# Gated layer: first projection as a Strassen block product, the second projection one token pair behind

## The chip, the cores and the metric

The kernel runs on one core of one Trainium2 chip. The time is device microseconds of one execution; lower is better. TensorE is called PE here, VectorE DVE, ScalarE ACT, GpSimd POOL, and SyncE, which issues most transfers, SP.

## The reference

One transformer block in float32, for 2 sequences of 1024 tokens and 256 features, with 154 condition tokens a sequence: self-attention, cross-attention, and a gated layer, each behind a layer norm and with a residual. The gated layer, cut to what matters:

```python
h = _layernorm(x, ln3_g, ln3_b)                 # 2 x 1024 x 256
p = h @ ff_w1 + ff_b1                           # 256 -> 2 x 1024
a, gate = (p[..., :D_FF], p[..., D_FF:])        # D_FF = 1024
h = a * jax.nn.gelu(gate, approximate=False) @ ff_w2 + ff_b2
x = h + x                                       # 1024 -> 256
```

## The kernel before

All three layers are written out in one program, and the order of the instructions on each engine is the order of the source. Every engine takes its own instructions strictly in that order. The outer loops run over p (self-attention steps), then c (48 cross-attention steps, three to a head pair), then k (64 slots of the gated layer). Short queues of closures spread the side work over the steps: `side` (the next layer norm, one step at a time), `outs` (pieces of an output projection, name py), `later` (loads and bias adds, L315), `adds`, `stores` and `lates` (what DVE, ACT or POOL do to a result one step later). The last cross-attention work reaches into the gated layer: the final softmax scaling (L824, POOL), transposes (L840, DVE), value products (poc, L876, PE) and their copies (L889, DVE), eight output pieces (L462, PE) with their residual adds (L469, DVE), and the third layer norm of the second sequence: statistics (L235, L236, DVE), deviation (L241, L245, POOL), the offset (L251, DVE), normalizing (L262, POOL), four PE transposes to a pair of token tiles (ph_ln, L275), and two ACT copies with gain and shift (L290).

The gated layer works on transposed activations hT (256 features as two chunks of 128 partitions, tokens along the free axis). A block is 256 tokens of one sequence; there are 8 blocks of 8 slots. `gate_slot(k)` makes one block of 128 features: four PE products of 128x128 weights and 256 tokens, two that sum up the gate half and two the linear half, in two halves of one PSUM tile pa from the pool ps_s (tiles of two banks of 512 float32, two of them). ACT applies Gelu with bias to the gate half (L964), then DVE adds the bias to the linear half and multiplies (L967) into u. `sum_slot()` comes at most some slots later: it multiplies that feature block with the second weights, one product for each of the two token tiles of the block, into two running sums (pf, pool ps_o, two banks). After the eighth feature block DVE adds each sum to the residual x (L993), and the result is stored. A float32 product is two weight loads and two matmul instructions on PE.

PSUM has two more banks in the pool ps_m (`mm_tile`). Before the change the gated layer's products don't use it; the output pieces, the value products and the norm's transposes do. SBUF tiles with the tag P (pool pp_) have six buffers.

The weights are laid out once, w1 as 2 chunks x 2048 columns, w2 as 8 blocks x 256, in one SBUF tile wf that is loaded in the cross-attention.

Of the kernel before, what the change touches and what calls it, by code (L numbers as in the profile page):

```python
# [8 lines left out]
F32 = mybir.dt.float32  # L9
AF = mybir.ActivationFunctionType  # L10
# [3 lines left out]
P = 128  # L14
# [4 lines left out]
def tile_transformer_block(ctx: ExitStack, tc: tile.TileContext, a: dict, out: bass.AP):  # L19
# [13 lines left out]
    GT = 4  # L33
# [884 lines left out]
            flush(stores)  # L918


    NBL = NT // TF
    FF = B * NBL * NF
    gated, sums = [], {}

    def hold_gated():

        wf = pt_.tile([P, 2 * NK, QH // 2], F32, tag="pT", name="wf").rearrange("p a b -> p (a b)")
        n1, n2 = NC * 2 * DF, NF * D
        w1 = wf[:, :n1].rearrange("p (c f) -> p c f", c=NC)
        w2 = wf[:, n1:n1 + n2].rearrange("p (f d) -> p f d", f=NF)  # L930
        pTc["pairs"] = wf[:, n1 + n2:n1 + n2 + 2 * NM * 2 * NT * KB].rearrange(
            "p (a m j q) -> p a m j q", a=2, m=NM, j=2)

        def part1(c, f):
            nc.sync.dma_start(out=w1[:, c, f:f + HB], in_=w["ff_w1"][c * P:(c + 1) * P, f:f + HB])

        def part2(f):
            nc.sync.dma_start(
                out=w2[:, f:f + 2, :],
                in_=w["ff_w2"][f * P:(f + 2) * P, :].rearrange("(f p) d -> p f d", p=P),  # L940
            )

        parts = [lambda c=c, f=f: part1(c, f) for c in range(NC) for f in range(0, 2 * DF, HB)]
        parts.extend(lambda f=f: part2(f) for f in range(0, NF, 2))
        return w1, w2, parts

    def gate_slot(k):

        blk, f = divmod(k, NF)
        b, t0 = divmod(blk * TF, NT)  # L950
        b1 = row_of["ff_b1"]
        h = hT["ff", b]
        if f == 0:
            sums[blk, "u"] = pt_.tile([P, NF, TF * P], F32, tag="V", name=f"u{blk}")
        pa = ps_s.tile([P, 2, HB], F32, tag="s", name=f"pa{k}")
        for half in (1, 0):
            for c in range(NC):
                nc.tensor.matmul(  # L958
                    pa[:, half, :TF * P],
                    lhsT=w1[:, c, half * DF + f * P:half * DF + (f + 1) * P],  # L960
                    rhs=h[:, c, t0 * P:(t0 + TF) * P], start=(c == 0), stop=(c == NC - 1),
                )
        gate = pp_.tile([P, TF * P], F32, tag="P", name=f"gate{k}")
        nc.scalar.activation(  # L964
            gate, pa[:, 1, :TF * P], AF.Gelu, bias=cols[:, b1 + NF + f:b1 + NF + f + 1]
        )
        nc.vector.scalar_tensor_tensor(  # L967
            sums[blk, "u"][:, f, :], pa[:, 0, :TF * P], cols[:, b1 + f:b1 + f + 1], gate,
            op0=ALU.add, op1=ALU.mult,
        )  # L970
        gated.append(k)

    def sum_slot():

        k = gated.pop(0)
        blk, f = divmod(k, NF)
        b, t0 = divmod(blk * TF, NT)
        if f == 0:
            sums[blk] = [sum_tile(f"pf{blk}_{i}") for i in range(TF)]
        for i in range(TF):  # L980
            nc.tensor.matmul(  # L981
                sums[blk][i][:, :D], lhsT=sums[blk, "u"][:, f, i * P:(i + 1) * P], rhs=w2[:, f, :],
                start=(f == 0), stop=(f == NF - 1),
            )
        if f < NF - 1:
            return None

        def store():
            n = TF if blk < B * NBL - 1 else 1
            for i in range(0, TF, n):  # L990
                for t in range(t0 + i, t0 + i + n):
                    xs = xt[b, t // GT][:, t % GT, :]
                    nc.vector.tensor_tensor(xs, sums[blk][t - t0][:, :D], xs, ALU.add)  # L993
                t = t0 + i
                (nc.scalar if i else nc.sync).dma_start(
                    out=out[b, t * P:(t + n) * P, :].rearrange("(t p) d -> p t d", p=P),
                    in_=xt[b, t // GT][:, t % GT:t % GT + n, :],
                )

        return store  # L1000


    with tc.manual_schedule():
# [98 lines left out]
        for c in range(CA):  # L1102
            if c == 0:
                pTc["ring"] = pt_.tile(
                    [P, 2 * NK, QH // 2], F32, tag="pT", name="pT_ca"
                ).rearrange("p a b -> p (a b)")[:, :3 * 2 * NB * NT * KB].rearrange(
                    "p (u n j q) -> p u n j q", u=3, n=NB, j=2)
            if c == SH + 1:
                out_pieces("sa", B - 1, NQ - 1, out_order("sa"))
            if c == SH + 1:  # L1110

                w1, w2, parts = hold_gated()
                add_biases("ca", 0)
# [24 lines left out]
            if c == 0:  # L1138
                drain.append(scale_groups(*joins.pop(0)))
            if c == 2:  # L1140
                turn_groups(SA - 1)
            cross_drain(c)
            if c == 1:
                run(lambda: cross_queries(*nxt))
            elif c == 2:
                run(lambda: cross_queries(*units[2], bank=sum_tile))
            elif c == 3:
                run(lambda: self_values(2 * NU - 1, 0))
            elif c == 4:
                run(lambda: self_values(2 * NU - 1, 1))  # L1150
            elif n == 0 and ui:
                if nxt:
                    run(lambda: cross_queries(*nxt))
                else:
                    run_work(2, 0)
                run_work(0, 1)
            elif n == 1:

                spare["turned"] = True
                run_work(0, 1, sum_tile if outs else None)  # L1160
                flush(stores)
                run_work(0, 0, n_sum=1)
                if ui % 2 == 0:
                    run(lambda: context_values(*units[ui]))
                run_work(1, 0)
                flush(adds)
                flush(stores)
                cross_weigh(c)
            elif n == 2:
                run_work(0, 1, sum_tile if ui == HP + 1 else None)  # L1170
                if c == SH + 1:
                    run_work(2, 0)
                elif ui == HP:
                    wo["ca"] = const.tile([P, NPAIR, D], F32, tag="wo", name="ca_wo")
                    later[:0] = [lambda i=i: nc.sync.dma_start(
                        out=wo["ca"][:, i, :], in_=w["ca_wo"][i * P:(i + 1) * P, :])
                        for i in range(NPAIR)]
            cross_regroup(c)
            for _ in range(min(2, len(later))):
                later.pop(0)()  # L1180

        spare["turned"] = False
        for k in range(FF):
            c = CA + k
            flush(adds)
            gate_slot(k)
            flush(stores)
            flush(lates)
            if k == 2 * len(CG) + 1:
# [1 line left out]
            if k == 0:  # L1191
                out_pieces("ca", B - 1, NQ - 2, out_order("ca"))
            cross_drain(c)
            cross_weigh(c)
            cross_regroup(c)
            if k == len(CG) + 2:
                out_pieces("ca", B - 1, NQ - 1, out_order("ca"))
            if k > len(CG) + 1:

                for _ in range(min(2, len(gated) - (1 if k < FF - 2 else 2))):  # L1200
                    run(sum_slot)
                flush(stores)

            run_work(0 if k == 1 else 2, 1)
            if later:
                later.pop(0)()
        while gated:
            run(sum_slot)
            flush(stores)


# [30 lines left out]
```

## Time and profile before

| | us |
|---|---|
| median of 3 runs | 1107.47 |
| lowest, highest | 1107.26, 1108.68 |
| span of the profiled execution, first to last instruction | 1106.7 |
| first product of the gated layer's first projection (L958) in it | starts at 915.1 |
| first product of the second projection (L981) | starts at 939.1 |

The profile is one execution. Its span covers the instructions alone; what lies around it in a timed run is not in the profile, so the median stands 0.8 us above the span. Groups of instructions are named by line, engine, operation and tiles (out<-in); PEld is the weight load of PE. For each group the profile gives busy time, the mean of one in ns, and the idle time of the engine just before it with the instruction that ended it.

### The profile page before, as it was taken

The page shows a single profiled execution, that of the slowest core. Times are in us where ns is not written, and L with a number is a line of the kernel's source. Part 1 is how long each engine was busy: PE and PEld are TensorE (multiplying, and loading weights), DVE is VectorE, ACT ScalarE, POOL GpSimd, SP SyncE. Part 2 cuts the span into 40 slices and gives each one's busy share as a digit, 9 for nine tenths or more (in the row PEclk, how much of TensorE's full clock was granted, in tenths as well). Part 3 has the DMA queues.
Part 4 walks back from the last instruction along what each step waited for, and adds up shares of the span by engine and source line. Part 5 has one row for each costly group of instructions (what it writes and reads, how often), then busy time and mean ns, then how long its engine had stood idle before and what let it go on. Part 6 is the DMA issues. An engine that isn't in the chain of part 4 may idle for free.

```text
span 1106.7 us, 44775 instructions
## 1 busy us (share of the span) xinstructions
PE 1088.1 (98%) x18452; PEld 721.6 (65%) x18452; DVE 854.5 (77%) x1205; ACT 624.6 (56%) x2025; POOL 662.2 (60%) x1456
## 2 busy tenths in 40 slices
PE   8999999999999999999999999999999999999998
PEld 6555656556756556566565565466776778888887
DVE  5899999898988999999999989868777885322222
ACT  4666666766666666667666766655556552121111
POOL 2766777777778777777777767666656653220000
PEclk9999999999999999999999999999999999999999
DMA  2222212121112022011111111136766553000000
GB/s 82 71 58 53 58 29 52 41 53 42 34 42 49 16 47 49 14 42 33 32 42 33 33 33 27 34 88 163 163 157 139 116 113 77 10 11 10 20 10 20
DMA packets 103982, 60.72 MB, mean 55 GB/s; under 512 B 32218, under 2 KB 94562, under 8 KB 103778
## 3 DMA queue, kind: packets, MB, share of 16 engines
q1 hardware_dynamic: 102546, 57.20, 21.8%
q8 instruction: 146, 2.39, 0.9%
q10 hardware_dynamic: 1232, 0.66, 0.2%
q14 instruction: 58, 0.48, 0.1%
HBM read 27.91 MB, written 2.10 MB: 27 GB/s over the span
## 4 chain that ended last, share of the span: by engine, by line
PE 70%; ACT 8%; DMA 7%; DVE 5%; POOL 4%; SPq 3%; issue 3%; DVEq 0%; POOLq 0%; ACTq 0%
PE po L534 13%; PE s L488 12%; PE pa L958 10%; ACT p L499 7%; DMA st<-st 6%; PE pf L981 5%; PE py_ca L462 5%; PE pq_ca L357 4%; PE poc L876 4%; PE py_sa L462 4%; SPq L509 3%; DVE st L649 3%; PE pv_sa L388 3%; PE sc L797 3%; PE pk_sa L357 3%
## 5 line engine op out<-in xcount | busy, mean ns | idle before, releaser
L499 ACT ACTIVATE p<-s,st 128x512 f32<-128x512 f32 x512 | 344.9, 686 | 196.6 <-DVE st L649 192.8
L599 POOL TENSOR_SCALAR p<-p,rd,ee 128x512 f32<-128x512 f32 x512 | 385.7, 768 | 48.3 <-DVE rd L595 47.4
L649 DVE TENSOR_REDUCE st<-s 128x2 f32<-128x1024 f32 x256 | 300.8, 1216 | 24.9 <-PE s L488 12.7
L613 DVE STREAM_TRANSPOSE pT<-p 128x1024 f32<-128x1024 f32 x256 | 302.4, 1219 | 0.2 <-POOL p L599 0.2
L488 PE MATMUL s<-k_sa,q_sa 64*32 64x512 f32 x4096 | 258.7, 592 | 7.2 <-ACT p L499 6.2
L534 PE MATMUL po<-pT,v_sa 64*32 64x256 f32 x8192 | 240.5, 378 | 1.7 <-DVE pT L613 1.4
L534 PEld LDWEIGHTS po<-pT,v_sa 64*32 64x32 f32 x8192 | 172.5, 107 | 78.7 <-issue 23.7
L488 PEld LDWEIGHTS s<-k_sa,q_sa 64*32 64x32 f32 x4096 | 80.6, 106 | 112.2 <-ACT p L499 51.6
L813 ACT ACTIVATE p<-sc,neg 128x154 f32<-128x154 f32 x256 | 96.1, 403 | 85.1 <-DVE rden L821 80.0
L824 POOL TENSOR_SCALAR p<-p,rden 128x154 f32<-128x154 f32 x256 | 96.8, 398 | 73.7 <-DVE rden L821 73.4
L967 DVE SCALAR_TENSOR_TENSOR u<-pa,cols,gate 128x256 f32<-128x256 f32 x64 | 31.0, 484 | 123.1 <-ACT gate L964 123.1
L958 PE MATMUL pa<-hT_ln,wf 128*128 128x256 f32 x512 | 121.1, 380 | 0.0
L964 ACT ACTIVATE gate<-pa,cols 128x256 f32<-128x256 f32 x64 | 30.3, 474 | 147.5 <-PE pa L958 144.2
L958 PEld LDWEIGHTS pa<-hT_ln,wf 128*128 128x128 f32 x512 | 96.7, 190 | 13.8 <-issue 0.9
L499 ACT ACTIVATION_READ_ACCUMULATOR p<-s,st 128x1 f32 x512 | 104.0, 203 | 0.0
L522 POOL TENSOR_TENSOR zz<-ee,st 128x8 f32<-128x8 f32 x128 | 25.9, 202 | 75.4 <-ACT ee L520 75.4
L388 PEld LDWEIGHTS pv_sa<-sa_wv,hT_ln 64*128 64x128 f32 x1024 | 58.8, 188 | 14.3 <-issue 5.0
L981 PE MATMUL pf<-wf,u 128*128 128x256 f32 x256 | 64.7, 379 | 0.0
L388 PE MATMUL pv_sa<-sa_wv,hT_ln 64*128 64x128 f32 x1024 | 62.0, 275 | 0.0
L462 PE MATMUL py_sa<-sa_wo,o_sa 128*128 128x256 f32 x256 | 59.7, 386 | 0.0
L462 PE MATMUL py_ca<-ca_wo,o_ca 128*128 128x256 f32 x256 | 59.7, 381 | 0.0
L462 PEld LDWEIGHTS py_sa<-sa_wo,o_sa 128*128 128x128 f32 x256 | 47.3, 190 | 17.8 <-ACT v_sa L397 5.9
(88 smaller groups left out, 1230.0 us busy)
## 6 DMA issues: line engine op xcount, KB each, us to landing
wf<-pT_ca SPq DMA_DIRECT2D x128, 128.0 KB, 2.4
st<-st SPq DMA_DIRECT2D x512, 1.0 KB, 1.8
v_sa<-v_sa SPq DMA_DIRECT2D x32, 256.0 KB, 3.8
sa_wq<-in_L_xattn_sa_wq_dram SPq DMA_DIRECT2D x32, 128.0 KB, 3.3
sa_wk<-in_L_xattn_sa_wk_dram SPq DMA_DIRECT2D x32, 128.0 KB, 2.7
sa_wv<-in_L_xattn_sa_wv_dram SPq DMA_DIRECT2D x32, 128.0 KB, 3.5
ca_wq<-in_L_xattn_ca_wq_dram SPq DMA_DIRECT2D x32, 128.0 KB, 3.9
wf<-in_L_xattn_ff_w_dram SPq DMA_DIRECT2D x12, 256.0 KB
```

Of the source, the lines that this page charges most:

```text
L388: nc.tensor.matmul(pv[r][:, i * P:(i + 1) * P], lhsT=h[own, c, i * P:(i + 1) * P], rhs=wt[own, c, :], start=(c == 0), stop=(c == NH - 1), ...
L462: nc.tensor.matmul(py[:, e * D:(e + 1) * D], lhsT=o[:, i, (t + e) * P:(t + e + 1) * P], rhs=wo[kind][:, g * HP + i, :], start=(i == 0), st ...
L488: nc.tensor.matmul(sc[a4 * KB:(a4 + 1) * KB, j, :], lhsT=q[r, c:c + KB], rhs=k[r, h * HB:(h + 1) * HB], start=True, stop=True, tile_positi ...
L499: nc.scalar.activation(pr[:, j, :], sc[:, j, :], AF.Exp, bias=st[:, 0, 0, i, j:j + 1], accum_out=st[:, 0, 1, i, j:j + 1],)
L534: nc.tensor.matmul(po[a2][d:d + KB, :QH // 2], lhsT=v[r, t, e, d:d + KB], rhs=pT[r, d // DH * NK + n, :], start=(t == 0 and e == 0), stop= ...
L599: nc.gpsimd.tensor_scalar(pr[:, j, :], pr[:, j, :], rd[:, c:c + 1], ee[:, 0, c:c + 1], op0=ALU.mult, op1=ALU.mult,)
L613: nc.vector.transpose(halves[h][:, :, c:c + KB], groups.pop(0).rearrange("p j (n k) -> p (j n) k", k=KB))
L649: nc.vector.tensor_reduce(st[:, 0, 0, i, :], sc[i], AX.X, ALU.max, negate=True)
L813: nc.scalar.activation(pr_[:, j, i, :T], sc[:, j, i * T:(i + 1) * T], AF.Exp, bias=neg[:, j, i:i + 1], accum_out=den[:, j, i:i + 1],)
L824: nc.gpsimd.tensor_scalar(pr_[:, j, i, :T], pr_[:, j, i, :T], rden[:, j, i:i + 1], 1.0, op0=ALU.mult, op1=ALU.mult,)
L958: nc.tensor.matmul(pa[:, half, :TF * P], lhsT=w1[:, c, half * DF + f * P:half * DF + (f + 1) * P], rhs=h[:, c, t0 * P:(t0 + TF) * P], star ...
L981: nc.tensor.matmul(sums[blk][i][:, :D], lhsT=sums[blk, "u"][:, f, i * P:(i + 1) * P], rhs=w2[:, f, :], start=(f == 0), stop=(f == NF - 1),)
```

## The change

The first projection is computed for 512 tokens of a sequence at a time (a pair of 256-token halves, 4 pairs, 8 feature blocks each: 32 units). For one feature block the gate and linear halves of the weights, the two feature chunks and the two token halves form a 2x2 block product. It is made with seven products (`product`, numbered 1 to 7) where there were eight. To that end:

- POOL makes sums and differences of the weights in the cross-attention's last 16 steps (`weight_sums`, 16 sums of 128x256; one of the three kinds is written back into w1), and for each pair four sums of token blocks are made (`token_sums`): by DVE for the first pair, at the end of the last cross-attention step, by POOL for the others, half a pair ahead.
- The loop has 64 half units. `gate_first(n)` issues product 1 into a bank of ps_m (pa), which ACT copies to SBUF (own 0); then, by `gate_last(n - 1)`, product 4 of the unit before; then 6 and 5 into the two halves of a ps_s tile pb, to each of which DVE adds own 0 (L1018, L1020). `gate_second(n)` accumulates product 2 onto pa (Gelu by ACT, L1032), product 7 onto the first half of pb (DVE adds own 2 and the bias, L1034), product 3 onto the second half (DVE, L1037; Gelu by ACT, L1038); POOL multiplies into u (L1039). Product 4 accumulates onto the first half of pb once more, DVE takes it (L1046), and POOL multiplies (L1048).
- The second projection starts when a pair's eight units are done, and runs through the next pair's units, two products a half unit, one token tile after the other; the last pair's 32 products come after the loop. Each token tile is added and stored by itself (L1071, L1072).
- u is kept for whole pairs, in the buffers of the tags V and oT and, once, over kT.
- `cross_weigh` runs only in the second half of a unit, and the side work's share of ps_m banks alternates between one and two a step.

```diff
+    def product(n, i, into, first):
+        pair, f = divmod(n, NF)
+        own = slice(f * P, (f + 1) * P)
+        lhs = {
+            1: w1[:, 0, 1, own], 2: w1[:, 1, 1, own], 3: wsum[4][:, own], 4: w1[:, 1, 0, own],
+            5: wsum[1][:, own], 6: wsum[2][:, own], 7: w1[:, 0, 0, own],
+        }[i]
+        nc.tensor.matmul(
+            into[:, :BT], lhsT=lhs, rhs=wh[pair][i], start=first, stop=True,
+            skip_group_check=True)
+
+    def gate_first(n):
...
+        own = pp_.tile([P, 4, BT], F32, tag="P", name=f"own{n}")
+        pa, pb = mm_tile(f"pa{n}"), ps_s.tile([P, 2, HB], F32, tag="s", name=f"pb{n}")
+        psum[n] = (pa, pb[:, 0, :], pb[:, 1, :], own)
+        product(n, 1, pa, True)
+        nc.scalar.copy(own[:, 0, :], pa[:, :BT])
+        if n:
+            gate_last(n - 1)
+        product(n, 6, psum[n][1], True)
+        nc.vector.tensor_tensor(own[:, 1, :], psum[n][1][:, :BT], own[:, 0, :], ALU.add)
+        product(n, 5, psum[n][2], True)
+        nc.vector.tensor_tensor(own[:, 2, :], psum[n][2][:, :BT], own[:, 0, :], ALU.add)
+
+    def gate_second(n):
...
+        product(n, 2, pa, False)
+        nc.scalar.activation(own[:, 3, :], pa[:, :BT], AF.Gelu, bias=bg)
+        product(n, 7, pb, False)
+        nc.vector.scalar_tensor_tensor(
+            own[:, 2, :], pb[:, :BT], ba, own[:, 2, :], op0=ALU.add, op1=ALU.add)
+        product(n, 3, pc, False)
+        nc.vector.tensor_tensor(own[:, 1, :], pc[:, :BT], own[:, 1, :], ALU.add)
+        nc.scalar.activation(own[:, 1, :], own[:, 1, :], AF.Gelu, bias=bg)
+        nc.gpsimd.tensor_tensor(ub[pair][1][:, f, :], own[:, 2, :], own[:, 1, :], ALU.mult)
+
+    def gate_last(n):
...
+        product(n, 4, pb, False)
+        nc.vector.scalar_tensor_tensor(
+            own[:, 0, :], pb[:, :BT], biases(n)[0], own[:, 0, :], op0=ALU.add, op1=ALU.add)
+        nc.gpsimd.tensor_tensor(ub[pair][0][:, f, :], own[:, 0, :], own[:, 3, :], ALU.mult)
+        if f == NF - 1:
+            sums.extend((pair, i, e) for i in range(2 * TF) for e in range(NF))
...
-        for k in range(FF):
+        for k in range(2 * FU):
             c = CA + k
             flush(adds)
-            gate_slot(k)
+            (gate_second if k % 2 else gate_first)(k // 2)
...
-            cross_weigh(c)
+            if k % 2:
+                cross_weigh(c - 1 if k == len(CG) + 2 else c)
...
-            if k > len(CG) + 1:
-                for _ in range(min(2, len(gated) - (1 if k < FF - 2 else 2))):
-                    run(sum_slot)
-                flush(stores)
-            run_work(0 if k == 1 else 2, 1)
+            if k % (2 * NF) == NF and k < 2 * FU - 2 * NF:
+                token_sums(k // (2 * NF) + 1, nc.gpsimd)
+            for _ in range(min(2, len(sums))):
+                run(sum_slot)
+            flush(stores)
+            run_work(0 if k == 1 else 1 + k % 2, 1)
             if later:
                 later.pop(0)()
-        while gated:
+        gate_last(FU - 1)
+        while sums:
             run(sum_slot)
             flush(stores)
```

More of the change, by code (lines that the diff above doesn't have):

```diff
@@ L918, in cross_weigh @@
             flush(stores)
-    NBL = NT // TF
-    FF = B * NBL * NF
-    gated, sums = [], {}
+    NPR = B * 2
+    BT = S // 4
+    FU = NPR * NF
+    wsum, wh, ub, psum = {}, {}, {}, {}
     def hold_gated():
@@ L928, in hold_gated @@
         n1, n2 = NC * 2 * DF, NF * D
-        w1 = wf[:, :n1].rearrange("p (c f) -> p c f", c=NC)
+        w1 = wf[:, :n1].rearrange("p (c h f) -> p c h f", c=NC, h=2)
         w2 = wf[:, n1:n1 + n2].rearrange("p (f d) -> p f d", f=NF)
@@ L932, in hold_gated, with part1 @@
             "p (a m j q) -> p a m j q", a=2, m=NM, j=2)
-        def part1(c, f):
-            nc.sync.dma_start(out=w1[:, c, f:f + HB], in_=w["ff_w1"][c * P:(c + 1) * P, f:f + HB])
+        def part1(c, h, f):
+            f0 = h * DF + f
+            nc.sync.dma_start(out=w1[:, c, h, f:f + HB], in_=w["ff_w1"][c * P:(c + 1) * P, f0:f0 + HB])
         def part2(f):
@@ L941, in part2 @@
             )
-        parts = [lambda c=c, f=f: part1(c, f) for c in range(NC) for f in range(0, 2 * DF, HB)]
+        parts = [
+            lambda c=c, h=h, f=f: part1(c, h, f)
+            for c in range(NC) for h in range(2) for f in range(0, DF, HB)
+        ]
         parts.extend(lambda f=f: part2(f) for f in range(0, NF, 2))
         return w1, w2, parts
[L947 to L951, printed above, removed]
-        h = hT["ff", b]
-        if f == 0:
[L954 to L965, printed above, removed]
-        )
[L967 to L984, printed above, removed]
+    def weight_sums(n):
+        if n == 0:
+            for i in (1, 2):
+                wsum[i] = p2.tile([P, DF], F32, tag="KT", name=f"w1s{i}")
+        if n == DF // (2 * P):
+            wsum[4] = p2.tile([P, DF], F32, tag="QT", name="w1s4")
+        f = n * 2 * P % DF
+        own = slice(f, f + 2 * P)
+        (g0, a0), (g1, a1) = ([w1[:, c, h, own] for h in (1, 0)] for c in range(NC))
+        s1, s2 = wsum[1][:, own], wsum[2][:, own]
+        tt = nc.gpsimd.tensor_tensor
+        if n < DF // (2 * P):
+            return [
+                lambda: tt(s1, a0, a1, ALU.add),
+                lambda: tt(s2, s1, g0, ALU.subtract),
+                lambda: tt(a0, g0, a0, ALU.subtract),
+            ]
+        return [lambda: tt(wsum[4][:, own], g1, s2, ALU.subtract)]
@@ new lines, in token_sums @@
+    def token_sums(pair, engine):
+        b, t0 = divmod(pair * 2 * BT, S)
+        h = hT["ff", b]
+        own = [[h[:, c, t0 + j * BT:t0 + (j + 1) * BT] for j in range(2)] for c in range(NC)]
+        t = pp_.tile([P, 3, BT], F32, tag="P", name=f"hs{pair}")
+        engine.tensor_tensor(t[:, 0, :], own[0][1], own[0][0], ALU.subtract)
+        engine.tensor_tensor(t[:, 1, :], own[1][1], t[:, 0, :], ALU.subtract)
+        engine.tensor_tensor(own[0][1], own[1][1], own[0][1], ALU.subtract)
+        engine.tensor_tensor(t[:, 2, :], own[1][0], t[:, 1, :], ALU.subtract)
+        wh[pair] = {
+            1: own[0][0], 2: own[1][0], 3: own[1][1], 4: t[:, 2, :],
+            5: t[:, 0, :], 6: t[:, 1, :], 7: own[0][1],
+        }
@@ new lines, in product @@
+    def product(n, i, into, first):
[9 more added lines that the diff above has]
+    def gate_first(n):
+        pair, f = divmod(n, NF)
+        if f == 0:
+            one_u = pt_.tile([P, NF, BT], F32, tag="oT" if pair % 2 else "V", name=f"u{pair}_0")
+            if pair == 0:
+                other = kT.rearrange("p a b -> p (a b)")[:, :NF * BT].rearrange(
+                    "p (f t) -> p f t", f=NF)
+            else:
+                other = pt_.tile([P, NF, BT], F32, tag="oT" if pair % 2 else "V", name=f"u{pair}_1")
+            ub[pair] = (one_u, other)
+        own = pp_.tile([P, 4, BT], F32, tag="P", name=f"own{n}")
[9 more added lines that the diff above has]
+        nc.vector.tensor_tensor(own[:, 2, :], psum[n][2][:, :BT], own[:, 0, :], ALU.add)
@@ new lines, in biases @@
+    def biases(n):
+        c = row_of["ff_b1"] + n % NF
+        return cols[:, c:c + 1], cols[:, c + NF:c + NF + 1]
+    def gate_second(n):
+        pair, f = divmod(n, NF)
+        pa, pb, pc, own = psum[n]
+        ba, bg = biases(n)
+        product(n, 2, pa, False)
[7 more added lines that the diff above has]
+        nc.gpsimd.tensor_tensor(ub[pair][1][:, f, :], own[:, 2, :], own[:, 1, :], ALU.mult)
@@ new lines, in gate_last, with sum_slot @@
+    def gate_last(n):
+        pair, f = divmod(n, NF)
+        pa, pb, pc, own = psum.pop(n)
+        product(n, 4, pb, False)
[4 more added lines that the diff above has]
+            sums.extend((pair, i, e) for i in range(2 * TF) for e in range(NF))
+    sums, summed = [], {}
+    def sum_slot():
+        pair, i, f = sums.pop(0)
+        if f == 0:
+            summed[pair] = sum_tile(f"pf{pair}_{i}")
+        own = summed[pair]
+        j, e = divmod(i, TF)
+        nc.tensor.matmul(
+            own[:, :D], lhsT=ub[pair][j][:, f, e * P:(e + 1) * P], rhs=w2[:, f, :],
+            start=(f == 0), stop=(f == NF - 1),
+        )
@@ L985, in sum_slot @@
         if f < NF - 1:
             return None
+        b, t = divmod(pair * 2 * TF + i, NT)
         def store():
[L989 to L998, printed above, removed]
+            xs = xt[b, t // GT][:, t % GT, :]
+            nc.vector.tensor_tensor(xs, own[:, :D], xs, ALU.add)
+            (nc.scalar if pair == NPR - 1 and i % 2 else nc.sync).dma_start(
+                out=out[b, t * P:(t + 1) * P, :], in_=xs)
@@ L1180, in tile_transformer_block @@
                 later.pop(0)()
+            if c == CA - 16:
+                weighted = [fn for n in range(4) for fn in weight_sums(n)]
+            if CA - 16 <= c < CA - 4:
+                weighted.pop(0)()
+            elif c >= CA - 3:
+                for n in {CA - 3: (4,), CA - 2: (5, 6), CA - 1: (7,)}[c]:
+                    weight_sums(n)[0]()
+            if c == CA - 1:
+                token_sums(0, nc.vector)
         spare["turned"] = False
-        for k in range(FF):
+        for k in range(2 * FU):
             c = CA + k
             flush(adds)
-            gate_slot(k)
+            (gate_second if k % 2 else gate_first)(k // 2)
             flush(stores)
```

## The prediction

> **What bounds the kernel now.** I read the busy shares first, then the slices, then the costliest groups of the stage that changes, then its timeline.
>
> ```profile
> PE 1088.1 (98%) x18452; PEld 721.6 (65%) x18452; DVE 854.5 (77%) x1205; ACT 624.6 (56%) x2025; POOL 662.2 (60%) x1456
> ...
> PE   8999999999999999999999999999999999999998
> ...
> DVE  5899999898988999999999989868777885322222
> ...
> POOL 2766777777778777777777767666656653220000
> PEclk9999999999999999999999999999999999999999
> ```
>
> PE is busy in every slice. In the last eight slices, the gated layer, DVE and POOL have little to do. There the matrix engine alone sets the time.
>
> ```profile
> L967 DVE SCALAR_TENSOR_TENSOR u<-pa,cols,gate 128x256 f32<-128x256 f32 x64 | 31.0, 484 | 123.1 <-ACT gate L964 123.1
> L958 PE MATMUL pa<-hT_ln,wf 128*128 128x256 f32 x512 | 121.1, 380 | 0.0
> L964 ACT ACTIVATE gate<-pa,cols 128x256 f32<-128x256 f32 x64 | 30.3, 474 | 147.5 <-PE pa L958 144.2
> ```
>
> The first projection is 256 products, each two PE instructions. PE never idles before one of them (0.0). DVE and ACT wait for PE, never PE for them: the pa tile gets its four products before anything reads it.
>
> ```profile
> 1042.88 1.89 PE L958 MATMUL pa<-hT_ln,wf 128*128 128x256 f32 x8
> 1044.60 1.03 PE L981 MATMUL pf<-wf,u 128*128 128x256 f32 x4
> 1045.47 1.89 PE L958 MATMUL pa<-hT_ln,wf 128*128 128x256 f32 x8
> ```
>
> A slot of 12 instructions takes 1045.47 - 1042.88 = 2.59 us. An instruction thus costs 0.216, a product 0.431, and a result lands 0.379 after its start (the row above says 380).
>
> **What is removed.** Seven products for eight over 512 tokens and 128 features: 32 products fewer of 256, 64 instructions x 0.216 = -13.8 us. The second projection keeps its 128 products. At the end one add and one store follow the last product instead of two adds (0.86 in the timeline for the pair): -0.4. Together **-14.2**.
>
> **What is added: waits of PE for DVE inside a unit.** A unit (one feature block of one 512-token pair) runs on PE as products 1, 4 of the unit before, 6, 5, two second-projection products, 2, 7, 3, two more. Product 6 fills one bank of the tile pb (two banks), 5 the other; DVE reads both (L1018, L1020); 7 and 3 accumulate onto them and are read again (L1034, L1037); then 4. In the built order, with its semaphore counts, product 5 waits for L1018, which reads product 6's bank, not its own. Likewise 7 waits for L1020, 3 for L1034, 4 for L1037. The tile is guarded as one, so neighbouring products alternate with DVE instead of streaming.
>
> [...]
>
> Price of one such turn, from PE's last start: 0.379 to the result; 0.05 until DVE starts (a result at 17.18 is taken by DVE at 17.25); 0.418 for an add from PSUM (the x<-pf,x row) or 0.484 for the three-operand form (L967); 0.12 until PE's next weight load (a DVE copy ends at 17.67, PE loads at 17.79); 0.10 until that load lets the product run (a lone group of eight lasts 1.99, a streaming one 1.89). Sum 1.07 or 1.13; streaming would have taken 0.216. So 3 after 7 loses 0.92. 5 after 6 loses 0.85, and as DVE handles product 4's result first, 0.07 more: 0.92. Waits of 7 and 4 come after 0.216 + 0.86 + 0.43 = 1.51 of other PE work where second-projection products stand between, and cost nothing. A unit so takes 22 x 0.216 + 1.84 = 6.6 us against 5.17 for two slots now.
>
> - **Units 8 to 31** (with second projection): 24 x 1.84 = **+44.2**.
> - **Units 4 to 7** have no second projection between, since it starts when the first pair is complete. All four waits bite: 0.92 + 0.42 + 0.92 + 0.42 = 2.68 a unit, 10.7. There the last norms run too. Their transposes use the same PSUM pair as product 1, and ACT empties them only behind the second Gelu. So product 1 of units 6 and 7 waits for add 0.418, Gelu 0.474 and the two copies (1.01 by the hT_ln rows of L290): with result, hand-overs and restart (0.379, 0.14, 0.22) 2.64 from product 3's last start, less 0.22 and 0.44 of PE work, 1.98 each, and spares a 0.42. 10.7 + 3.96 - 0.84 = **+13.8**. POOL too has a chain there: 1.6 until its first input, then four token sums, five products and a bias add at 0.73 (the x<-x,ff_b row), four times 0.90 for the deviations (0.19 + 0.71) and four times 1.10 to normalize: 16.9 us from the start of unit 4 to the last transpose. A streaming PE would be there after 21 products and three transposes, 10.4; the PE slowed as above comes at about 20, so POOL adds nothing.
> - **Units 0 to 3.** Product 6 needs token sums that DVE makes behind the transposes ending at 917.23: two adds at 0.418 (no row has both inputs in SBUF; 0.3 to 0.45 bounds them), to 918.1, plus restart 0.22, where PE would come at 915.6: 2.7. The rest of unit 0: 0.9 (product 5), 0.2, and 1.3 (product 3's reader behind two transposes). After the next weighing product 1 waits for a copy out of its bank: 0.85; the last out pieces now stand right behind their weighing: 0.9. Three units at 1.84: 5.5. Sum **+12.4**.
> - **Weight sums:** 16 POOL sums x 0.73 = 11.7 us in the last 16 cross steps, hidden: POOL waits 53.5 us there for reciprocals. Uncovered, the four in the last three steps would cost up to 3. I take 0. No DMA is added before the end; 16 small stores take the place of 8 with SP's queue empty.
>
> Extra DVE work a unit (five PSUM reads, 2.2 us), ACT (1.3) and POOL (1.5) fit in 6.6 us.
>
> **Sum:** -14.2 + 44.2 + 13.8 + 12.4 = +56.2 on the span of 1106.7: 1162.9. The median of the runs, 1107.47, lies 0.8 above the profiled span: **1163.7 us**, 5% slower.
>
> **Bounds.** No row shows a turn inside an accumulation. If the weight load runs ahead and the restart is nearly free (0.05 for 0.22), a turn loses 0.17 less: 1.5 a unit, and some 70 turns less 12 us: 1152. If DVE's adds run 10% longer beside POOL and the weight sums bite: 2.0 a unit, 5 more, 3 more, and the POOL chain adds 5: 1177. I take the middle, as the restart rows are of this kernel's own PE.
>
> **Would the clock fall?** PE would have a quarter of its time idle in gaps under 1 us.
>
> ```profile
> 32.00:36.00 4.00, 2.41 (x48) 0.75 (x40) 2.55 (x4) 2.38 (x8) 1.69 (x6) 1.00 0.21 59
> ```
>
> The row is a stretch of 4 us near the start (PE, PEld, DVE, ACT, POOL busy, then the granted clock): PE busy 60%, clock 1.00. So I price no loss. [...]
>
> **Rivals.**
> - *PE keeps streaming* (faster): the reads always end before the next product, so only the -14.2 stays: 1093.3. For it: DVE is idle most of the stage. Against it: product 5 starts 0.216 after 6's last instruction, while a read needs 0.85. It decides where a turn loses under 14.2 / 64 = 0.22 us instead of 0.92.
> - *Only true bank conflicts bind* (no change): if the cross-bank waits cost nothing, POOL's chain becomes the limit of units 4 to 7 (16.9 - 10.4 = 6.5, and 1.98 for ACT's copies) and the start stays (2.7 + 0.85 + 0.9): 1107.5 - 14.2 + 8.5 + 4.5 = 1106.3. Against: the waits are in the program.
> - *Turns half hidden*: 1.0 a unit, 1130 to 1150, if weight loads and decode overlap fully and DVE starts at once. The rows at 17.2 to 17.8 speak against.
> - *The clock drops* in the gaps: if a quarter of the stage's 448 + 256 instructions took double, 176 x 0.216 = 38 more, 1202; with less or more of it 1180 to 1230. The 32 to 36 us row speaks against; its stretch is short.
>
> **How the numbers follow.** Main case 0.80, half hidden 0.08, clock 0.07, streaming 0.03, no change 0.02. The range 1150 to 1180 takes the bounds, leaving out 0.20. Slower by over 0.2% (2.2 us, about what a measurement here can tell) is 0.95, within 0.02, faster 0.03.
>
> **What would show it.** In the profile after: the idle of PE or its weight loads before the products' line released by L1018 and L1034, some 28 us each; steps of 6.6 us from one unit to the next in the late stretch; second-projection products still at 0.216; PE busy near three quarters of the last slices; DVE no longer waiting for ACT but PE for DVE. Steps of 4.7 us would prove me wrong on the waits, steps of 5.7 on their price, a granted clock below 0.95 on the clock.

## The result, and the profile after

The changed kernel takes **1168.47 us** (median of four runs, 1164.85 to 1175.66) beside 1108.08 for the kernel before in the same comparison: a ratio of 1.055, interval 1.052 to 1.059, or 60.4 us more. The forecast was 1163.7 with a range of 1150 to 1180, and slower with a chance of 0.95.

The busy shares and slices of the changed kernel's profile (its span of 1173.9 us is that of the slowest of the four runs):

```profile
PE 1110.9 (95%) x18388; PEld 717.6 (61%) x18388; DVE 899.2 (77%) x1305; ACT 638.2 (54%) x2057; POOL 731.7 (62%) x1548
...
PE   8999999999999999999999999999999887888888
...
DVE  4889999898899999999999898787787643333332
...
PEclk9999999999999999999999999999999896999999
```

PE runs 64 instructions less than before, and yet it is no longer busy throughout: from slice 32 on it stands at seven or eight tenths, with no other engine near its limit. Two slices show a granted clock below nine tenths, which the profile of before has nowhere.

Three of PE's groups from unit 8 on (1001 to 1174 us). The last column is PE's idle time just before the group and what ended it:

```profile
L1061 PE MATMUL pf<-wf,u 128*128 128x256 f32 x224 | 55.0, 379 | 0.0
L995 PE MATMUL pb<-hs,w1s 128*128 128x256 f32 x96 | 31.5, 410 | 14.1 <-DVE own L1018 14.1
L995 PE MATMUL pb<-hT_ln,w1s 128*128 128x256 f32 x48 | 16.8, 431 | 13.8 <-DVE own L1034 13.8
```

Before, PE never idled ahead of a product of the first projection. Here all of its idle time ends with two reads by DVE: L1018, which holds up product 5, and L1034, which holds up product 3. These are the two waits that the prediction named. They are 14 us each on PE, and 24.1 and 23.5 on its weight loads, where the prediction looked for some 28 each. The second projection (L1061) still has none. One such turn, from the timeline of all engines:

```profile
1015.32 0.59 PE L995 MATMUL pb<-hs,w1s 128*128 128x256 f32 x2
1015.52 0.48 DVE L1046 SCALAR_TENSOR_TENSOR own<-pb,cols,own 128x256 f32<-128x256 f32 x1 [0.44 <-PE pb L995]
1016.02 0.42 DVE L1018 TENSOR_TENSOR own<-pb,own 128x256 f32<-128x256 f32 x1
...
1016.50 0.30 PEld L995 LDWEIGHTS pb<-hs,w1s 128*128 128x128 f32 x2 [0.99 <-DVE own L1018]
1016.50 0.70 PE L995 MATMUL pb<-hs,w1s 128*128 128x256 f32 x2 [0.59 <-DVE own L1018]
```

Product 6 starts at 1015.32, its second instruction 0.216 later, at 1015.54. DVE first finishes with product 4 (L1046), then reads product 6's bank until 1016.44. Only then does product 5 start, at 1016.50, though it writes the other bank. From the last start to the next are 0.96 us where streaming has 0.216, and a group behind such a restart lasts 0.70 for 0.59. One turn so costs 0.75 + 0.11 = 0.86 us. A unit with its two turns takes 6.45 us (product 5 at 1010.05 and at 1016.50).

Where the clock fell, in windows (start and end, length, PE's busy time and instructions, granted clock, DMA share, GB/s): units 0 to 3, 4 to 7, and 8 to 31.

```profile
918.77:965.53 46.76, 38.36 (x221) 0.89 0.20 42
965.53:1000.22 34.69, 26.25 (x73) 0.65 0.00 0
1000.22:1156.28 156.06, 128.13 (x530) 0.99 0.03 10
```

Units 8 to 31 lost next to nothing to the clock (0.99); units 4 to 7 ran 24 of their 35 us at half clock.

To see where the time went, the gated layer can be cut at the first products of units 4 and 8, as the timelines give them. The first row is worked out: the 191.6 us of before less 64 x 0.2156; of it 24 x 22 x 0.2156 = 113.8 and the 17.6 from the last product 4 to the end for units 8 to 31, and 28 x 0.431 + 4 x 0.44 (a group of four transposes in the profile of before) for units 4 to 7. The second adds the stalls of the prediction. The others are measured, in microseconds.

| | units 0–3 | units 4–7 | unit 8 to the end | sum |
|---|---|---|---|---|
| streaming (worked out) | 32.6 | 13.8 | 131.4 | 177.8 |
| predicted | 45.0 | 27.6 | 175.2 | 247.8 |
| changed kernel, this profile | 46.8 | 34.7 | 173.7 | 255.1 |
| changed kernel, second profile (e7_after) | 45.7 | 28.4 | 172.7 | 246.8 |
| one-bank tiles (e1_single) | 43.1 | 24.3 | 131.5 | 198.9 |
| sums and norm moved (e2_early) | 45.8 | 22.7 | 173.2 | 241.7 |
| both (e3_both) | 42.6 | 14.7 | 132.4 | 189.7 |
| both and the start (e5_start), from the end of the last scores | 33.5 | 14.7 | 132.5 | 180.7 |

The table compares the gated layer alone, because its start moves from profile to profile, in no order that follows the edits: 915.1 us before, 918.8 in the changed kernel, 914.3 in its second profile. The kernel before took 1111.18 us beside e1 to e4, 1109.08 beside e5 to e7 and 1108.76 beside e8. Ratios are therefore given, each to the kernel before beside the same runs.

### The profile page after: what moved, and what is told of

It is laid out like the page before. It is cut to its first block, busy times and chain, and to the rows that moved or that the text cites. A ratio compares the mean times of both kernels' runs of the same rounds, so it can differ in the third digit from the quotient of the medians.

```text
span 1173.9 us, 44881 instructions
## 1 busy us (share of the span) xinstructions
PE 1110.9 (95%) x18388; PEld 717.6 (61%) x18388; DVE 899.2 (77%) x1305; ACT 638.2 (54%) x2057; POOL 731.7 (62%) x1548
## 4 chain that ended last, share of the span: by engine, by line
PE 61%; DVE 10%; ACT 9%; DMA 7%; POOL 6%; SPq 4%; issue 4%; DVEq 0%; POOLq 0%; ACTq 0%
PE s L488 10%; PE po L534 10%; ACT p L499 8%; PE pb L995 7%; DMA st<-st 6%; PE pf L1061 5%; PE py_ca L462 4%; PE pq_ca L357 4%; DVE st L649 4%; PE poc L876 3%; SPq L509 3%; PE py_sa L462 3%; PE pv_sa L388 3%; PE sc L797 3%; PE pa L995 3%
## 5 line engine op out<-in xcount | busy, mean ns | idle before, releaser
L499 ACT ACTIVATE p<-s,st 128x512 f32<-128x512 f32 x512 | 345.4, 687 | 195.7 <-DVE st L649 189.7
L649 DVE TENSOR_REDUCE st<-s 128x2 f32<-128x1024 f32 x256 | 300.9, 1216 | 25.4 <-PE s L488 10.5
L488 PE MATMUL s<-k_sa,q_sa 64*32 64x512 f32 x4096 | 262.3, 594 | 9.0 <-ACT p L499 8.0
L1039 POOL TENSOR_TENSOR u<-own 128x256 f32<-128x256 f32 x24 | 17.5, 728 | 99.6 <-ACT own L1038 99.6
L1032 ACT ACTIVATE own<-pa,cols 128x256 f32<-128x256 f32 x32 | 15.2, 474 | 101.9 <-PE pa L995 101.9
L995 PE MATMUL pb<-hs,w1s 128*128 128x256 f32 x128 | 45.0, 435 | 21.4 <-DVE own L1018 18.9
L357 PE MATMUL pq_sa<-hT_ln,sa_wq 64*32 64x512 f32 (+1 forms) x976 | 59.3, 594 | 0.0
L357 PE MATMUL pq_ca<-hT_ln,ca_wq 64*128 64x512 f32 (+1 forms) x304 | 58.6, 590 | 0.3 <-DVE rden L821 0.3
```

What stands on the lines that cost most here:

```text
L357: nc.tensor.matmul(pq[r][f:f + m, at:at + n], lhsT=wt[own, c, f:f + m], rhs=h[own, c, t0:t0 + n], start=(c == 0), stop=(c == NH - 1), tile ...
L488: nc.tensor.matmul(sc[a4 * KB:(a4 + 1) * KB, j, :], lhsT=q[r, c:c + KB], rhs=k[r, h * HB:(h + 1) * HB], start=True, stop=True, tile_positi ...
L499: nc.scalar.activation(pr[:, j, :], sc[:, j, :], AF.Exp, bias=st[:, 0, 0, i, j:j + 1], accum_out=st[:, 0, 1, i, j:j + 1],)
L649: nc.vector.tensor_reduce(st[:, 0, 0, i, :], sc[i], AX.X, ALU.max, negate=True)
L995: nc.tensor.matmul(into[:, :BT], lhsT=lhs, rhs=wh[pair][i], start=first, stop=True, skip_group_check=True)
```

## The experiments

**e1_single: is it the guard of the two-bank tile?** From unit 2 on the halves of pb are tiles of their own:

```diff
-        pa, pb = mm_tile(f"pa{n}"), ps_s.tile([P, 2, HB], F32, tag="s", name=f"pb{n}")
-        psum[n] = (pa, pb[:, 0, :], pb[:, 1, :], own)
+        pa = mm_tile(f"pa{n}")
+        if n < 2:
+            pb = ps_s.tile([P, 2, HB], F32, tag="s", name=f"pb{n}")
+            psum[n] = (pa, pb[:, 0, :], pb[:, 1, :], own)
+        else:      # the pool ps_s is closed here, ps_g: four tiles of one bank
+            psum[n] = (pa, *(ps_g[0].tile([P, HB], F32, tag="g", name=f"{name}{n}")
+                             for name in ("pb", "pc")), own)
```

> The changed kernel with one edit: from the third unit on, the two halves of pb are two separate one-bank tiles, so that product 5 no longer waits for the read behind product 6, nor 3 for the read behind 7. Theory (the guard of the two-bank tile costs most of the loss): units 8 to 31 lose 24 x 1.7 us of idle and come at about 4.75 us a unit where the changed kernel took 6.45; what is left is the start (some 8 us) and the norm's POOL chain in units 4 to 7 (some 8 us), so 1107.5 - 14.2 + 8 + 8 + 0.9 = about 1110, up to 1120 if the granted clock still falls there. Rival (the stalls come from PE and DVE sharing the two banks of one tile's region or from DVE itself, not from the guard): steps stay near 6.4 us and the time stays at 1160 or more. Rival (half of the gain is lost to new waits on the own bank): steps of 5.5 us, about 1130.

Measured: 1119.29 us, ratio 1.007 (1.005 to 1.009). PE's groups from unit 8 on, the same two products as above:

```profile
L997 PE MATMUL pc<-hT_ln,w1s 128*128 128x256 f32 x50 | 14.9, 379 | 0.0
L997 PE MATMUL pc<-hs,w1s 128*128 128x256 f32 x48 | 14.3, 379 | 0.0
```

The idle time of 28 us is gone to the last tenth, and a unit takes 4.75 us (its first products at 1040.26 and 1045.01). So the waits of these units were the guard's alone: the same instructions in the same order, with PE writing one bank while DVE reads another, take 4.75 us where 22 x 0.2156 = 4.74 is streaming. What is left of the loss stands in units 0 to 7. In units 4 to 7, two rows of PE's timeline show it:

```profile
968.25 0.33 PE L277 MATMUL ph_ln<-ident,xn_ln 128*128 128x128 f32 x1 [3.88 <-POOL xn_ln L264]
...
974.08 0.70 PE L997 MATMUL pa<-hT_ln,wf 128*128 128x256 f32 x2 [1.33 <-ACT hT_ln L292]
```

The turns between PE and DVE had hidden POOL's chain of sums and norm steps. Without them PE reaches the transposes 3.9 us early, and the copies of ACT hold up product 1 of the next unit.

**e2_early: the other costs alone.** pb stays one tile. The moves:

```diff
-            if c == CA - 1:
+            if c == CA - 2:
                 token_sums(0, nc.vector)
...
-            if k % (2 * NF) == NF and k < 2 * FU - 2 * NF:
+            if k in (3, 24, 40):
...
-            run_work(0 if k == 1 else 1 + k % 2, 1)
+            if k < 8:
+                run_work(0 if k == 1 else 1 + k % 2, 1)
+            else:
+                run_work(1 + k % 2, k % 2, sum_tile if k < 16 else None)
```

> The changed kernel with pb as it is, but the other costs moved: the first pair's token sums one cross-attention step earlier, the second pair's sums in slot 3 in place of 8, the last norm one step every second slot from slot 8, with its transposes in the second projection's idle banks up to slot 15. Theory (the guard carries most of the loss, the start and the norm the rest): units 8 to 31 stay at 6.45 us; 1 to 2.5 us go at the start and 5 to 8 in units 4 to 7, and where the long PE idles go, the stretches at half the granted clock go with them (some 8 to 15 us of the changed kernel's runs): 1145 to 1160. Rival (start and norm chain carry most of the loss): below 1130. Rival (the bank waits alone bring the clock down): stretches at half clock remain in units 4 to 7, 1155 to 1165.

Measured: 1161.58 us, ratio 1.045 (1.043 to 1.046), just above the range expected. Units 8 to 31 did not move. Units 4 to 7, in windows:

```profile
963.49:986.22 22.73, 16.66 (x66) 1.00 0.00 0
```

They fell by 12 us against the first profile of the changed kernel and by 5.7 against the second, and the clock stays full there though all four bank waits remain. So here the bank waits alone did not bring the clock down (1.00), and the norm and its sums cost nothing behind unit 7. Units 0 to 3 gained 1 us against the first profile and nothing against the second, where 1 to 2.5 were expected, and the half clock at the start stayed, for two windows. Product 5 of unit 0 waits 3.55 us there, for the reason that the next run shows.

**e3_both.** The two edits together.

> Both edits together: one-bank tiles from the third unit, and token sums and norm steps moved. Theory: only the removed products and the rest of the start stay, 1107.5 - 14.2 + 5 + 1 + 0.9 = about 1100, between 1096 and 1106, faster than before the change; units at 4.75 us throughout. Rival (another engine or own-bank waits become the bound): units above 5.2 us and 1107 or more.

Measured: 1111.25 us, ratio 1.000 (0.998 to 1.001), a miss: units 4 to 31 run as expected, but the start did not mend. The timeline of the start, some rows:

```profile
918.99 0.83 DVE L981 TENSOR_TENSOR hs<-hT_ln,hs 128x256 f32<-128x256 f32 x1
...
920.42 0.79 DVE L804 TENSOR_REDUCE neg<-sc 128x4 f32<-128x616 f32 x1
...
921.30 0.39 ACT L815 ACTIVATE p<-sc,neg 128x154 f32<-128x154 f32 x1 [3.40 <-DVE rden L823]
...
922.77 0.38 ACT L1021 COPY own<-pa 128x256 f32<-128x256 f32 x1
...
923.19 0.42 DVE L1025 TENSOR_TENSOR own<-pb,own 128x256 f32<-128x256 f32 x1 [0.77 <-ACT own L1021]
...
923.67 1.22 PE L997 MATMUL pb<-hs,w1s 128*128 128x256 f32 x2 [3.03 <-DVE own L1025]
```

The sums, one step earlier, now stand in front of DVE's maximum of the last scores (L804, L802 before), which begins at 920.42; in the changed kernel it began 0.12 us after the start of unit 0's first product, here 1.86. The last exponentials come later by that, the copy of product 1 (L1021) stands behind them on ACT, and product 5 behind the read that needs the copy. The wait of 2.5 us for the sums became one of 0.7, but product 5's wait grew from 0.6 to 3.0: the step had been moved to a worse place in DVE's queue.

**e4_wsums: are the weight sums free?** The kernel before, with the 16 POOL sums added at their places:

```diff
+            if c == CA - 16:
+                weighted = [fn for n in range(4) for fn in weight_sums(n)]
+            if CA - 16 <= c < CA - 4:
+                weighted.pop(0)()
+            elif c >= CA - 3:
+                for n in {CA - 3: (4,), CA - 2: (5, 6), CA - 1: (7,)}[c]:
+                    weight_sums(n)[0]()
```

> The kernel before with the 16 sums of weights added on POOL at the places where the changed kernel has them, into tiles that nothing reads. Theory (POOL waits there for reciprocals, the sums are hidden): 1107.5, within 0.5. Rival (the sums delay the scaling of the last softmax steps): 1109 to 1111, with PE waiting for transposes that wait for POOL in the last three cross-attention steps.

Measured: 1111.68 us beside 1111.18, ratio 1.0005 (0.9992 to 1.0018). The gated layer starts at 918.5 there and takes 191.7 us, as before. A cost of more than 2 us is excluded, one of 0.5 is not.

**e5_start: the two edits and a start put in order.** The first pair's sums are made behind the fourth cross-attention step from the end, unit 0 has its two sums in two tiles of ps_s, and ps_g opens with unit 1. Further:

```diff
+            if k == 0:
+                out_pieces("ca", B - 1, NQ - 2, out_order("ca"))
+                run_work(1, 1, sum_tile)
...
-            if k == 0:
-                out_pieces("ca", B - 1, NQ - 2, out_order("ca"))
             cross_drain(c)
             if k % 2:
                 cross_weigh(c - 1 if k == len(CG) + 2 else c)
+            if k == 1:
+                gate_last(0)
```

> Both edits of the last run, and the start rearranged: the first pair's token sums four cross-attention steps before the end, one output piece and the last transposes ahead of unit 0's first product, unit 0's two sums in two tiles, product 4 of unit 0 behind the value products, the one-bank tiles from unit 1. Theory (what is left of the loss lies at the start: PE waits 0.7 us for the token sums, 3.0 for the copy behind the last exponentials, some 2.5 for half clock after that, 1.2 for two turns): units 0 to 3 fall from 42.6 us to about 35, the time to 7 to 8 us under the kernel before, a ratio of 0.993. Rival (the moved sums and pieces only wait elsewhere, or delay the last softmax steps): units 0 to 3 at 40 or more, or the gated layer begins 2 us later, a ratio of 0.998 or above.

Measured: **1099.26 us, ratio 0.990 (0.989 to 0.992)**: faster than both kernels, and 9.8 us under the kernel before where 7 to 8 were expected. PE's timeline at the start:

```profile
915.12 0.63 PE L277 MATMUL ph_ln<-ident,xn_ln 128*128 128x128 f32 x4
915.69 2.00 PE L464 MATMUL py_ca<-ca_wo,o_ca 128*128 128x256 f32 x8
917.52 0.59 PE L997 MATMUL pa<-hT_ln,wf 128*128 128x256 f32 x2
917.95 0.59 PE L997 MATMUL pb<-hs,w1s 128*128 128x256 f32 x2
918.41 0.70 PE L997 MATMUL pc<-hs,w1s 128*128 128x256 f32 x2
918.95 0.60 PE L997 MATMUL pa<-hT_ln,wf 128*128 128x256 f32 x2
```

The last transposes and one output piece cover the time in which DVE and ACT finish the last softmax step, and the first products follow without a gap. From the end of the last scores to the end of the kernel are 180.7 us, 10.9 less than before, where streaming would give 13.8 less. By the table, 0.9 of the missing 2.9 lie in units 0 to 3, 0.9 in units 4 to 7 and 1.1 behind. The clock is full from there to the end (1.00 from 900 to 1095). The parts of the rearranged start were not run one by one, so what each is worth is not shown.

**e6_gaps: what lowers the clock?** The kernel before, in which PE is made to wait at known places:

```diff
+        own = h[:, :, t0 * P:(t0 + TF) * P]
+        for _ in range({18: 1, 23: 3, 28: 6, 33: 1, 38: 3, 43: 6}.get(k, 1 if 51 <= k < 62 else 0)):
+            nc.vector.tensor_scalar(own, own, 1.0, 1.0, op0=ALU.mult, op1=ALU.mult)
```

> The kernel before with PE made to wait in the gated layer: VectorE multiplies a token block by 1 in place (once, three or six times) between two slots that read it, so that PE idles about 0.9, 1.9 and 3.4 us in slots 18 to 43, twice each, far apart; slots 51 to 61 have one such wait each. Theory (one idle of over two us is what brings the granted clock down): about half clock for some us after the long idles alone, none in slots 51 to 61. Rival (the share of idle over several us counts): half clock in slots 51 to 61 too, where PE idles a quarter of the time. Rival (idle time of this size does not move the clock; the stretches have another cause): 1.00 everywhere. The time is about 20 to 30 us above the kernel before in any case.

Measured: 1136.12 us, one run. The idles were 0.70, 1.57, 2.95 and again 1.31, 1.57, 2.95 us, and 0.65 every 3.5 us later on (one of 1.31). The clock fell behind the two of 2.95 and nowhere else. Windows around the first 1.57 and the first 2.95:

```profile
999.21:1002.62 3.41, 2.21 (x10) 1.00 0.00 0
1012.86:1016.27 3.41, 0.74 (x4) 1.00 0.00 0
1016.27:1019.69 3.42, 3.14 (x8) 0.50 0.00 0
1019.69:1023.10 3.41, 3.41 (x17) 1.00 0.02 5
```

The stretches at 0.50 last 3.41 us, and their starts (1016.27 and 1064.06) lie 47.8 us apart, 14 times 3.41. The other profiles agree: the starts of their stretches lie 14 (e1), 16 (both profiles of the changed kernel), 17 and 22 (e8) such windows apart, each within 0.05 us. So in each of these profiles the falls lie on one grid of 3.41 us.

**e8_share: single idle or share of a window?** Short idles packed closely, with the second projection put off in the slots concerned:

```diff
+    paused = {k: n for k0, n in ((18, 2), (34, 1), (50, 2)) for k in range(k0, k0 + 5)}
...
         for half in (1, 0):
+            for _ in range(paused.get(k, 0)):
+                nc.vector.tensor_scalar(own, own, 1.0, 1.0, op0=ALU.mult, op1=ALU.mult)
...
-                for _ in range(min(2, len(gated) - (1 if k < FF - 2 else 2))):
+                for _ in range(0 if k in paused else min(2, len(gated) - (1 if k < FF - 2 else 2))):
```

> The kernel before with short waits packed closely: in slots 18 to 22, 34 to 38 and 50 to 54 the second projection is put off to later slots, and VectorE multiplies the token block by 1 in place ahead of each half of the four products (twice in the first and third group of slots, once in the second), so that PE works 0.86 us and idles about 1.2, or 0.8, in turn. Theory (the clock is set in windows of 3.41 us, and one in which PE is busy 0.52 or less is followed by half clock, one with 0.55 or more is not): half clock inside the first and third group, where PE is busy some 0.42 of a window though no idle exceeds the 1.57 us that left the clock alone in the run with single waits; none or a short one in the second group, at about 0.52; the stretches last multiples of 3.41 us. Rival (only a single idle of two to three us counts): 1.00 in all three groups. The time is some 10 to 25 us above the kernel before.

Measured: 1182.97 us, one run, 74 us above the kernel before, where 10 to 25 were expected; the clock was at half for 25 windows, ten, six and nine in the three groups. Windows of the grid, around the first fall, the recovery, and the fall in the second group:

```profile
982.91:986.32 3.41, 1.26 (x6) 1.00 0.00 1
986.32:989.74 3.42, 1.82 (x4) 0.50 0.00 0
...
1017.04:1020.46 3.42, 3.42 (x9) 0.50 0.00 0
1020.46:1023.87 3.41, 3.41 (x17) 1.00 0.00 0
1054.59:1058.00 3.41, 1.90 (x8) 1.00 0.00 0
1058.00:1061.41 3.41, 1.38 (x6) 1.00 0.00 0
1061.41:1064.83 3.42, 2.90 (x7) 0.50 0.00 0
```

The first group falls with idles of 1.17 and 0.98, the second with none over 1.51: shorter than the 1.57 that left the clock alone. So in these two runs the length of an idle does not tell the windows ahead of a fall from the others, and PE's busy share of a window does. The window with 1.90 of 3.41 busy (0.56) was followed by full clock, that with 1.38 (0.40) by half. The second group was expected to fall briefly or not at all. Its idles came out at 0.52 and 1.51 us in turn instead of about 0.8, and it stayed low for six windows. The third group fell like the first, behind a window with 1.13 of 3.41 busy (0.33).

**e7_after: the changed kernel once more.**

> The changed kernel itself on the chip of these runs, for a second look at its clock. Theory (the half-clock stretches come with the start and with units 4 to 7 and vary in length from run to run): a ratio of 1.045 to 1.06, 0.50 granted after unit 0's first idle and in units 4 to 7, none behind unit 9. Rival (one disturbed run): 1.00 throughout and a ratio near 1.043.

Measured: 1164.91 us, ratio 1.051 (1.048 to 1.054). The half clock comes at the same two places, after unit 0's first idle and in units 4 to 7, but for two windows and one, where the first profile has three and eight.

## Why the prediction was right, step by step

- **What bounds, and the waits**: right. e1 takes the guard away and with it all idle time behind unit 8; e2 leaves it and nothing there changes. The rivals "streaming" and "only true conflicts" fell with the first profile, and so did "turns half hidden": a unit loses 1.71 us to its two turns, not 1.0.
- **The price of a turn** was 0.92 and is 0.86. The mis-sized term is the 0.12 from DVE's end to PE's next weight load: here it is 0.06 (1016.44 to 1016.50). Units of 6.45 for 6.6, and 41.3 to 42.3 us for 44.2. The upper bound let DVE's adds run 10% longer beside POOL, which no run shows: in the changed kernel the add of L1018 took 0.41 to 0.43 us in all 32 units, where 0.418 had been taken.
- **Units 4 to 7**: of the 13.8, the guard's share (9.9 with the spared waits) is 8.9 in e2 (22.7 - 13.8). The norm's 4.0 is 5.7 (28.4 - 22.7), with one window at half clock in it. That POOL adds nothing held but for 1.0 us of waits for L262. Its chain alone, priced at 8.5 with ACT's copies, shows in e1: 24.3 - 13.8 = 10.5, again with a half-clock window.
- **Units 0 to 3**: 12.4 predicted, 13.1 in the second profile, 14.2 in the first, half clock included. The wait for the token sums is 2.52 (2.7 less restart), as worked out, but two errors cancel in it: the two sums took 0.48 and 0.50 us, above the prediction's bound of 0.45, and PE started 0.15 behind them where 0.22 was taken.
- **Weight sums**: nothing, as taken (e4). **The removed products**: e5 gets 10.9 of the 13.8. **The last 0.4**, one add for two behind the last product, did not come: 3.2 us from the last product's end in both profiles.
- **The clock** is the step that failed. "So I price no loss" went by a row of 4 us with PE busy 60% and by gaps under 1 us. But the prediction's own sum had a wait of 2.7 us at the start and ones of 1.98 in units 6 and 7, and the clock fell behind windows that were emptier than that row: PE was busy 0.40 of the time at the start and 0.52 in units 4 to 7 (last section). By the prediction's sign, a granted clock below 0.95, units 0 to 3 (0.89) and 4 to 7 (0.65) went wrong, units 8 to 31 (0.99) did not. The loss was there in both profiles: 37.5 us at half clock in the first, 10.2 in the second. The gated layers differ by 8.3 us over these 27.3, so 0.30 for each. By this estimate, which rests on two profiles, 3 to 11 us were missing from the sum. The timed runs agree in direction: of the eight of the changed kernel, the one with the lowest granted clock (0.983) took the longest, 1175.66 us, and the one with the highest (0.996) took 1162.91. The rival that priced the loss at 38 was too dear: it thought of a quarter of the stage's instructions, and only the start and units 4 to 7 were hit. That work takes double at a granted 0.50 is measured: in units 4 to 7 the starts of two products that follow without a wait lie 0.86 us apart (982.11 and 982.97), for 0.43 at 1.00. The profile of before has one such stretch too, ahead of the gated layer: 3.41 us from 721.56 on, behind 3.41 us in which PE was busy 1.66 (0.49).

Without the half clock the gated layer would have come to about 246.8 - 3.1 = 243.7, 4 less than predicted, so it is partly luck that the sum came out so close: the waits had been priced too high and the clock at nothing. Beside the kernel before, the runs of the first comparison are 60.4 us longer by their medians and those of e7 55.8, where the sum had 56.2. Of the 12 us by which the first profile's run (1175.66) lies above the forecast, 7.3 are in the gated layer, 3.7 arose ahead of it, and 1.0 lies outside the span.

In the first profile the clock fell at two places: at the start behind an idle of 2.52 us, and in units 4 to 7 behind idles of 0.84 and less. The steady units, with an idle of 0.59 twice in 6.45 us, kept 1.00.

## What to carry to other kernels

Before a chain of accumulations is split over the halves of one PSUM tile, read in the built order which waits it gets: a guard on the tile as a whole turned two independent chains into one that alternates between PE and DVE, at 0.86 us a turn, and two tiles of one bank each took all of it away in units 8 to 31. A stall hides the next one: without the bank waits POOL's norm chain came out, without that the last softmax step, and only when all three were dealt with did the removed products show. A step moved earlier is paid by whatever stands behind it in the new place.

## What was not expected of the hardware

In the gated layer of seven profiles (both of the changed kernel, e1, e2, e3, e6, e8) the granted clock fell to 0.50 thirteen times, and each stretch lasted one, two, three, six, eight, nine or ten times 3.41 us. Cut into windows of that length along the falls, each of the seven shows the same: every window at full clock in which PE was busy up to 0.52 of the time was followed by half clock (0.15 in e1 to 0.52 in the changed kernel and e2), and none in which it was busy 0.55 or more (0.55 in e7, 0.56 in e8). From the changed kernel, the window ahead of the fall at the start (0.40), the one ahead of the long stretch (0.52) with the first of that stretch, and the last of the stretch with the one behind it:

```profile
918.11:921.52 3.41, 1.36 (x11) 1.00 0.92 199
...
972.72:976.14 3.42, 1.78 (x8) 1.00 0.01 2
976.14:979.55 3.41, 2.83 (x9) 0.50 0.00 0
...
1000.03:1003.44 3.41, 2.99 (x7) 0.50 0.02 5
1003.44:1006.86 3.42, 2.68 (x11) 1.00 0.00 0
```

Back to full clock it went behind windows busy 0.86 to 1.00, and once behind one of 0.80, while others of 0.80 to 0.85 stayed low. So in the changed kernel half clock outlasted the low window: between waits for DVE and ACT its PE came to 0.67 to 0.83 in seven such windows on end, all at 0.50. The shares go by busy times with modelled ends, and the windows by the falls themselves; what sets the clock is not shown beyond these profiles.
